# Joining two visits of layer 0's values on TensorE, and moving three steps around them

## The chip, the cores and the metric

The kernel runs on one core of one Trainium2 chip. The metric is the time of one execution on the device in microseconds; lower is better. Times are given as the median of a few runs. A profile is one further execution, recorded by the hardware.

A core has several engines that run side by side and wait for each other through semaphores: TensorE (PE, matrix products, with weight loads counted apart as PEld), VectorE (DVE), ScalarE (ACT), GpSimd (POOL), and SyncE (SP), which here issues the DMA transfers. Each engine takes its instructions in the order of the program.

## The reference, cut to what matters

64 graphs of 256 nodes with 512 features each, an adjacency matrix for each graph, 8 heads of 64. Two layers follow each other; each ends in a residual sum and a layer norm.

```python
# layer 0: graph attention with additive logits
feats  = einsum('bnf,hfu->bhnu', X, W)
e_self, e_neigh = feats . a_self, feats . a_neigh
dense  = leaky_relu(e_self[:, None] + e_neigh[None, :], 0.2) - 1e10 * (1 - A)
out    = relu(softmax(dense) @ feats + b)
x      = layernorm(x + out)
# layer 1: dot-product attention plus adjacency and distance terms
q, k, v = split(x @ W_qkv)
attn   = 0.33 * softmax(q k^T / 8) + 0.33 * adj + 0.33 * exp(-adj)
x      = layernorm(x + (attn @ v) @ W_out + b_out)
```

## The kernel before, in words

All arithmetic is in float32, and everything of one graph stays in SBUF. The 64 graphs pass through a software pipeline written out by hand: in stage b, layer 0's attention of graph b stands beside layer 1's projections of graph b-1 (`attention0_beside_projections1`, L1141), and then layer 1's attention of graph b-1 and b-2 stands beside layer 0's projection of graph b+1 (`attention1_beside_projections0`, L1220). `start()` (L1047) does graph 0 in another way, since the weights of layer 1 are still on their way and layer 0's attention vectors have still to be folded into its weights. `end()` empties the pipeline. The function `do` (L1039) emits one step and then calls `in_order` (L86), which chains every new instruction to the one before it on its engine: the order in the source is the order on each engine.

**Seven products for eight.** The projections of both layers use a Strassen-like scheme of seven block products p1 to p7 (`seven`, L289). Three PSUM banks hold them (L284): p1, p6, p7 and p4 accumulate one on the other in the bank "chain", and after each one ScalarE copies the bank out (L309); p2 has the bank "alone"; p5 and then p3 accumulate in the bank "pair". VectorE adds "alone" or "pair" to what was copied (L312): add 11 uses p2, add 22 uses p5, add 12 uses p5 and p3. So p4 may begin only when p7's copy is out, and p3 only when add 22 has read the bank. For q and k (`pq_p`) a product is 16 records of 128 columns; for v (`pv_p`) and for layer 0 (`pf_p`) it is 4 records of 256 and 264 columns.

**Layer 0's attention.** The exponential of a sum of two logits is split in a row factor and a column factor. `rows` (L482) transposes the row logits with TensorE (four records, `pr`), takes their maximum, exponentiates them (ScalarE, L491), clips them (VectorE, L494) and sends the row to DRAM and back as a broadcast to all partitions (tiles `gs` and `gb`, SP, L498 and L499). `columns` (L541) starts with the subtraction `nd` (VectorE, L543), which waits for that broadcast, and ends in two exponentials on ScalarE. For each of 8 heads, `scaled` multiplies the features by the column factor (ScalarE, two instructions, L610) and `weights` builds the masked weights `pT` (VectorE, two instructions, L646). `product(g, t)` (L657) multiplies weights and features on TensorE for four heads and one tile of 128 nodes: 32 records that use the array as two halves of 64 columns each. `norm0` (L677) divides by the sums, `end` adds the residual.

**Layer 1's attention.** `scores` (TensorE L813, ScalarE L822), `both` (VectorE L834), `sums` (TensorE L842, `pd`), `invert` (VectorE, L863 to L875, then `rs` and `rb`, a second broadcast through DRAM); two graphs later `weights` (VectorE, L901 and L908), `values` (TensorE L918), `residual` (VectorE L996) and `project` (TensorE L1003, with its sum on VectorE, L931).

The order of one stage today, where the change touches it: q/k p1, p2, `columns`, p6, scaling and weights of heads 0 to 3, the store of graph b-3 (two normalisations on ScalarE, L367), add 11, p5, p7, add 22, `product(0, .)`, scaling of heads 4 to 7, p4, weights of heads 4 to 7, `norm0(0, .)`, `attend1` weights 0, p3, add 12, load of a later graph, `product(1, .)`, v's p1, p2, `norm0(1, .)`. The tiles `pT` of all heads rotate through four buffers of one tag.

Of the kernel before, what the change touches and what calls it, by code (L numbers as in the profile page):

```python
# [8 lines left out]
FT = mybir.dt.float32  # L9
BF = mybir.dt.bfloat16  # L10
U8 = mybir.dt.uint8
AF = mybir.ActivationFunctionType
# [5 lines left out]
def kernel(  # L18
# [410 lines left out]
    def proj0(b):  # L429
# [52 lines left out]
        def rows():  # L482
            pr = ps_tile([H, 2, N], f"pr_{b}")
            for s in range(2):
                for t in range(T):
                    transpose(pr[:, s, t * P : (t + 1) * P], V0[b][:, t, :, U + s])
            grow = small.tile([H, N + 1], FT, tag="grow", name=f"grow_{b}", bufs=1)
            nb = small.tile([H, 1], FT, tag="nb", name=f"nb_{b}", bufs=2)
            nc.vector.tensor_reduce(grow[:, N : N + 1], pr[:, 1, :], AX.X, ALU.max)
            nc.vector.tensor_scalar_mul(nb, grow[:, N : N + 1], -0.8)  # L490
            nc.scalar.activation(  # L491
                grow[:, :N], pr[:, 0, :], AF.Exp, bias=nb, scale=-0.8
            )
            nc.vector.tensor_scalar(  # L494
                grow[:, :N], grow[:, :N], 1.0, TINY, op0=ALU.min, op1=ALU.max
            )
            gs = dram.tile([H, N + 1], FT, tag="gs", name=f"gs_{b}")
            nc.sync.dma_start(gs, grow)  # L498
            nc.sync.dma_start(  # L499
                gb.rearrange("p h n -> p (h n)"),  # L500
                gs.rearrange("h n -> (h n)").partition_broadcast(P),
            )
# [105 lines left out]
        def scaled(h):  # L608
# [16 lines left out]
            xT_rows=from_rows,  # L625
            aT=lambda: transpose_blocks(pa, ADJB[b]),
            rows=rows,
            columns=columns,
            far=far,
            shared=shared,  # L630
# [7 lines left out]
    def attend0(b):  # L638
        pT = {}

        def weights(h):

            tag = "pT" if b > 1 or h < HG else "p" if h < HG + 2 else "both"
            pT[h] = work.tile([P, T, N], FT, tag=tag, name=f"pT_{b}_{h}", bufs=4)
            for j in range(T):
                nc.vector.scalar_tensor_tensor(  # L646
                    pT[h][:, j, :],
                    GB[b][h],
                    CCOL[b][:, j, h : h + 1],
                    AT[b][:, j, :],  # L650
                    op0=ALU.max,
                    op1=ALU.mult,
                )

        AV = {}

        def product(g, t):  # L657


            if t == 0:  # L660
                AV[g] = psum.tile([P, T, F], FT, tag="sc", name=f"av0_{b}_{g}", bufs=2)
            av = AV[g][:, t, : HG * UA].rearrange("p (h u) -> p h u", u=UA)
            half = P // 2
            for k in range(HG):
                h = g * HG + k
                for j in range(T):
                    for r in range(2):
                        i = t * P + r * half
                        matmul(  # L669
                            av[r * half : (r + 1) * half, k, :],  # L670
                            pT[h][:, j, i : i + half],
                            V0[b][:, j, h, :UA],
                            start=(j == 0),
                            stop=(j == T - 1),
                        )

        def norm0(g, t):  # L677
            if b not in X1:
                X1[b] = io.tile([P, T, F], FT, tag="x1", name=f"x1_{b}", bufs=3)
            av = AV[g][:, t, : HG * UA].rearrange("p (h u) -> p h u", u=UA)  # L680
            rec = small.tile([P, HG], FT, tag="rec", name=f"rec0_{b}_{g}_{t}")
            nc.vector.reciprocal(rec, av[:, :, U])
            s = slice(g * HG * U, (g + 1) * HG * U)
            nc.vector.tensor_mul(
                X1[b][:, t, s].rearrange("p (h u) -> p h u", u=U),
                av[:, :, :U],
                rec.unsqueeze(2).to_broadcast([P, HG, U]),
            )

        def end(ts=slice(0, T)):  # L690
            if ts.start == 0:
                NORM["l0", b] = LayerNorm(X1[b], b, "l0")
            ln = NORM["l0", b]
            for t in range(ts.start, ts.stop):
                nc.vector.scalar_tensor_tensor(
                    X1[b][:, t, :],
                    X1[b][:, t, :],
                    0.0,
                    X[b][:, t, :],
                    op0=ALU.max,  # L700
                    op1=ALU.add,
                    accum_out=ln.sums[:, t : t + 1],
                )
            ln.mean(ts)
            if ts.stop == T:
                X.pop(b)

        return dict(
            weights=weights,
            product=product,  # L710
            norm0=norm0,
            end=end,
            squares=lambda *ts: NORM["l0", b].squares(*ts),
            norm=lambda *ts: NORM["l0", b].apply(*ts),
        )
# [323 lines left out]
    def do(stage, b, step, *args):  # L1039

        if 0 <= b < NB:
            if (stage, b) not in S:
                S[stage, b] = stages[stage](b)
            S[stage, b][step](*args)
            in_order()

    def start():  # L1047
# [12 lines left out]
        attention_vectors(0, 0)  # L1060
        attention_vectors(1, 0)
        do("proj0", 0, "maxima")
        attention_vectors(0, 1)
        do("turned", 1, "xT")
        do("proj0", 0, "columns")
        do("proj0", 0, "factors")
        attention_vectors(1, 1)
        attention_vectors(0, 2)
        attention_vectors(1, 2)
        attention_vectors(2, 0)  # L1070
        attention_vectors(3, 0)
        for h in range(2):
            do("proj0", 0, "scaled", h)
            do("attend0", 0, "weights", h)
        attention_vectors(2, 1)
        attention_vectors(3, 1)
        attention_vectors(2, 2)
        attention_vectors(3, 2)
        for h in range(2, HG):
            do("proj0", 0, "scaled", h)  # L1080
            do("attend0", 0, "weights", h)
        do("proj0", 1, "features", 0, 0)
        do("proj0", 1, "features", 0, 1)
        do("attend0", 0, "product", 0, 0)
        do("attend0", 0, "product", 0, 1)
        for h in range(HG, H):
            do("proj0", 0, "scaled", h)
            do("attend0", 0, "weights", h)
        do("proj0", 1, "features", 1, 0)
        do("attend0", 0, "product", 1, 0)  # L1090
        do("attend0", 0, "product", 1, 1)
        do("proj0", 1, "features", 1, 1)
        do("attend0", 0, "norm0", 0, 0)
        do("attend0", 0, "norm0", 0, 1)
        combine_weights1(0)
        do("attend0", 0, "norm0", 1, 0)
        do("attend0", 0, "end", tiles[0])
        do("attend0", 0, "squares", tiles[0])
        do("attend0", 0, "norm0", 1, 1)
        do("attend0", 0, "end", tiles[1])  # L1100
        do("attend0", 0, "squares", tiles[1])
        do("attend0", 0, "norm", tiles[0])
        for t in range(T):
            for g in range(2):
# [36 lines left out]
    def attention0_beside_projections1(b):  # L1141


        if b > 1:
# [9 lines left out]
            do("proj1", b - 1, "qk_add", 11)  # L1154
            do("proj1", b - 1, "qk", "p5")
            do("proj1", b - 1, "qk", "p7")
            do("proj1", b - 1, "qk_add", 22)
        do("attend0", b, "product", 0, 0)
        do("attend0", b, "product", 0, 1)
        if b > 1:  # L1160
            for h in range(HG, H):
                do("proj0", b, "scaled", h)
            do("proj1", b - 1, "qk", "p4")
            for h in range(HG, H):
                do("attend0", b, "weights", h)
        do("attend0", b, "norm0", 0, 0)
        do("attend0", b, "norm0", 0, 1)
        do("attend1", b - 2, "weights", 0)
        if b > 1:
            do("proj1", b - 1, "qk", "p3")  # L1170
            do("proj1", b - 1, "qk_add", 12)
        else:
            do("turned", b + 1, "xT")
            do("turned", b + 1, "xC")
            do("proj0", b, "shared")
# [3 lines left out]
            in_order()  # L1179
        if b + 2 < NB:  # L1180
            load(b + 2)
        do("attend0", b, "product", 1, 0)
        do("attend0", b, "product", 1, 1)
        do("proj1", b - 1, "values", "p1")
        do("proj1", b - 1, "values", "p2")
        do("attend0", b, "norm0", 1, 0)
        do("attend0", b, "norm0", 1, 1)
# [1 line left out]
        do("proj1", b - 1, "v_add", 11)  # L1189
        do("proj1", b - 1, "values", "p6")  # L1190
        do("proj1", b - 1, "values", "p5")
        do("attend1", b - 2, "weights", 1)
        do("proj1", b - 1, "values", "p7")
        do("proj1", b - 1, "v_add", 22)
        do("proj0", b + 1, "product", "p1")
# [24 lines left out]
    def attention1_beside_projections0(b):  # L1220
# [10 lines left out]
        for g in range(HG):  # L1231
            do("attend1", b - 2, "values", g)
        do("softmax1", b - 1, "scores", 2)
        do("softmax1", b - 1, "both", 2)
        do("softmax1", b - 1, "scores", 3)
        do("softmax1", b - 1, "both", 3)
        do("attend1", b - 2, "residual")
        do("attend1", b - 2, "project", 0)
        do("proj0", b + 1, "rows")
        do("proj1", b, "hT")  # L1240
        do("attend1", b - 2, "project", 1)
        do("softmax1", b - 1, "sums")
# [119 lines left out]
```

## Time and profile before

| | us |
|---|---|
| median of 3 runs | 2990.16 (2987.5 to 2992.53) |
| profiled execution, its own time | 2991.16 |
| its span in the profile | 2989.4 |
| TensorE busy | 2957.4 |
| VectorE busy | 2610.0 |
| ScalarE busy | 1478.2 |

In the lines of the profile a time in us from the span's start comes first, then the time that the group of instructions took, the engine, the line of the kernel, the operation, output and inputs, shapes and the count; in square brackets stands how long the engine sat idle before it and what released it. In the list of waits the three numbers are the total in us, the number of times and the longest. The busy share of TensorE counts overlapping matmuls once and says little on how well it is used; the distance from one instruction's start to the next says more.

### The profile page before, as it was taken

The page shows a single profiled execution, that of the slowest core. Times are in us where ns is not written, and L with a number is a line of the kernel's source. Part 1 is how long each engine was busy: PE and PEld are TensorE (multiplying, and loading weights), DVE is VectorE, ACT ScalarE, POOL GpSimd, SP SyncE. Part 2 cuts the span into 40 slices and gives each one's busy share as a digit, 9 for nine tenths or more (in the row PEclk, how much of TensorE's full clock was granted, in tenths as well). Part 3 has the DMA queues.
Part 4 walks back from the last instruction along what each step waited for, and adds up shares of the span by engine and source line. Part 5 has one row for each costly group of instructions (what it writes and reads, how often), then busy time and mean ns, then how long its engine had stood idle before and what let it go on. Part 6 is the DMA issues. An engine that isn't in the chain of part 4 may idle for free.

```text
span 2989.4 us, 64730 instructions
## 1 busy us (share of the span) xinstructions
PE 2957.4 (99%) x25526; PEld 2332.6 (78%) x25526; DVE 2610.0 (87%) x5151; ACT 1478.2 (49%) x3585; POOL 183.5 (6%) x526
## 2 busy tenths in 40 slices
PE   8899999999999999999999999999999999999998
PEld 7777877877878778778778778788787787787775
DVE  5889888889888888888888888888988988888885
ACT  2454554455455455455545544554554555455443
POOL 0000000000000000000000000000000000000000
PEclk7999999999999999999999999999999999999999
DMA  6353454444444444444534544444444435445431
GB/s 120 86 128 99 109 130 98 111 126 104 111 122 103 116 109 107 125 102 110 129 96 109 133 97 111 122 104 115 110 108 123 108 105 129 97 108 133 96 93 50
DMA packets 760613, 328.22 MB, mean 110 GB/s; under 512 B 693516, under 2 KB 694268, under 8 KB 744312
## 3 DMA queue, kind: packets, MB, share of 16 engines
q1 hardware_dynamic: 758200, 323.55, 43.5%
q8 instruction: 204, 3.34, 0.5%
q14 instruction: 97, 0.79, 0.1%
q10 hardware_dynamic: 2112, 0.52, 0.1%
HBM read 256.13 MB, written 67.61 MB: 108 GB/s over the span
## 4 chain that ended last, share of the span: by engine, by line
PE 92%; DVE 3%; DMA 3%; ACT 1%; issue 1%; SPq 0%; POOL 0%; DVEq 0%; POOLq 0%
PE pq_p L300 25%; PE po L1003 14%; PE pf_p L300 13%; PE pv_p L300 12%; PE pz L813 8%; PE av L669 8%; PE av L918 7%; PE pd L842 2%; DMA gb<-gs 1%; PE pr L82 1%; DMA out_dram<-x 1%; DVE p L908 0%; DVE p L901 0%; PE pg L532 0%; DMA gs<-grow 0%
## 5 line engine op out<-in xcount | busy, mean ns | idle before, releaser
L300 PE MATMUL pq_p<-hC,wqk_sb 128*128 128x128 f32 x4096 | 487.1, 277 | 2.0 <-ACT qk L309 1.9
L300 PEld LDWEIGHTS pq_p<-hC,wqk_sb 128*128 128x128 f32 x4096 | 468.9, 192 | 7.7 <-ACT qk L309 2.9
L1003 PE MATMUL po<-wo_sb,oT 128*128 128x512 f32 x1024 | 466.3, 599 | 0.0
L646 DVE SCALAR_TENSOR_TENSOR pT<-gb,ccol,at 128x256 f32<-128x256 f32 x992 | 403.2, 480 | 17.6 <-ACT ccol L550 17.6
L300 PEld LDWEIGHTS pq_p<-hT,wqk_sb 128*128 128x128 f32 x3072 | 355.9, 193 | 29.6 <-DVE hC L278 23.9
L300 PE MATMUL pq_p<-hT,wqk_sb 128*128 128x128 f32 x3072 | 373.6, 278 | 3.2 <-DVE hT L121 1.9
L822 ACT ACTIVATE p<-pz,hide 128x512 f32<-128x512 f32 x512 | 310.8, 691 | 123.9 <-PE av L918 106.7
L1003 PEld LDWEIGHTS po<-wo_sb,oT 128*128 128x128 f32 x1024 | 184.7, 190 | 207.5 <-issue 205.8
L309 ACT COPY v<-pv_p 128x256 f32<-128x256 f32 x256 | 95.5, 373 | 472.6 <-PE pv_p L300 472.5
L351 ACT ACTIVATE junk<-x,nmean_l 128x512 bf16<-128x512 f32 x256 | 185.6, 725 | 279.9 <-POOL nmean_l L346 275.8
L908 DVE TENSOR_TENSOR p<-p,ct 128x1024 f32<-128x1024 f32 x252 | 308.7, 1225 | 8.6
L901 DVE TENSOR_TENSOR p<-p,rb 128x1024 f32<-128x1024 f32 x252 | 304.5, 1208 | 5.2 <-DMA rb<-rs 5.2
L669 PE MATMUL av<-v,pT 128*64 128x65 f32 x8192 | 267.1, 223 | 0.6 <-DVE pT L646 0.6
L669 PEld LDWEIGHTS av<-v,pT 128*64 128x64 f32 x8192 | 249.3, 138 | 16.5 <-issue 1.4
L610 ACT ACTIVATE v<-v 128x64 f32<-128x64 f32 x1024 | 260.3, 342 | 0.0
L813 PE MATMUL pz<-qk 64*128 64x256 f32 x2048 | 256.2, 389 | 0.6 <-ACT p L822 0.5
L300 PE MATMUL pf_p<-wf_sb,xC 128*128 128x264 f32 x992 | 252.3, 387 | 0.0
L300 PE MATMUL pv_p<-wv_sb,hC 128*128 128x256 f32 x1024 | 244.4, 381 | 5.5 <-DVE v L312 5.3
L813 PEld LDWEIGHTS pz<-qk 64*128 64x128 f32 x2048 | 187.1, 186 | 65.1 <-ACT p L822 25.6
L918 PE MATMUL av<-p,v 128*64 128x256 f32 x2016 | 231.7, 382 | 0.0
L300 PEld LDWEIGHTS pv_p<-wv_sb,hC 128*128 128x128 f32 x1024 | 193.4, 190 | 37.8 <-DVE v L312 10.7
L309 ACT COPY qk<-pq_p 128x512 f32<-128x512 f32 x256 | 147.7, 577 | 141.5 <-PE pq_p L300 141.4
(137 smaller groups left out, 3806.2 us busy)
## 6 DMA issues: line engine op xcount, KB each, us to landing
rb<-rs SPq DMA_DIRECT2D x63, 1024.0 KB, 4.6
gb<-gs SPq DMA_DIRECT2D x62, 1028.0 KB
xb<-in_x_dram SPq DMA_DIRECT2D x252, 128.0 KB, 4.1
x<-in_x_dram SPq DMA_DIRECT2D x63, 512.0 KB
hs<-x SPq DMA_DIRECT2D x63, 512.0 KB
hb<-hs SPq DMA_DIRECT2D x252, 128.0 KB, 3.4
out_dram<-x SPq DMA_DIRECT2D x63, 512.0 KB, 4.4
adj<-in_adj_dram SPq DMA_DIRECT2D x256, 64.0 KB, 4.5
```

Source lines behind the costliest of these rows:

```text
L300: matmul(d, lhsT, rhs, start=(p in FIRST and i == 0), stop=(i == len(todo) - 1), skip_group_check=True,)
L309: nc.scalar.copy(out[COPIES[p]], dst)
L351: nc.scalar.activation(junk, self.src[:, t, :], AF.Square, bias=self.nmean[:, t : t + 1], accum_out=self.rstd[:, t : t + 1],)
L610: nc.scalar.activation(V0[b][:, t, h, :U], V0[b][:, t, h, :U], AF.Copy, scale=V0[b][:, t, h, U : U + 1],)
L646: nc.vector.scalar_tensor_tensor(pT[h][:, j, :], GB[b][h], CCOL[b][:, j, h : h + 1], AT[b][:, j, :], op0=ALU.max, op1=ALU.mult,)
L669: matmul(av[r * half : (r + 1) * half, k, :], pT[h][:, j, i : i + half], V0[b][:, j, h, :UA], start=(j == 0), stop=(j == T - 1),)
L813: matmul(pz[:, r, j, :], QK[b][rows, g, 1, j * P : (j + 1) * P], QK[b][rows, g, 0, :], start=True, stop=True,)
L822: nc.scalar.activation(p[:, :, j, :], pz[:, :, j, :], AF.Exp, bias=hide[:, j, b : b + 1], scale=U**-0.5,)
L901: nc.vector.tensor_mul(p, p, REC[b][:, k : k + 2, g // 2, :] .unsqueeze(2) .to_broadcast([P, 2, T, N]),)
L908: nc.vector.tensor_add(p, p, CT[b].unsqueeze(1).to_broadcast([P, 2, T, N]))
L918: matmul(av[0][r * U : (r + 1) * U, g % 2, :], V1[b][:, j, 2 * g + r, :], PROBS[b][g][:, r, j, :], start=(j == 0), stop=(j == T - 1),)
L1003: matmul(po, oT[:, c, t * P : (t + 1) * P], wo_sb[:, c, :], start=(c == 0), stop=(c == C - 1),)
```

## The change

Three edits, in the author's words: layer 0's values in one visit with v's first product between q and k's last; row logits ahead of output; the first graph's values ahead of columns.

1. In the stage of graph b (b > 1), the weights of heads 4 to 7 now follow p7 directly, ahead of add 22. After add 22 come `attend1` weights 0, v's p1, then q/k p4 and p3 and add 12, and only then all four `product` steps, one after the other. `attend1` weights 1 move from between v's p5 and p7 to behind the products, ahead of `norm0`. So that eight weight tiles can live at once, heads 4 to 7 use the buffers of the tag "both".
2. `rows` is cut in two. The transposes and the maximum now come right behind the last scores, ahead of `both` 2 and 3; the new step `broadcast` (exponential, clip, the two DMAs) comes behind `both` 3 and ahead of `residual` and `project(0)`. Before, all of it stood behind `project(0)`.
3. In `start()`, graph 0's scaling, weights, values, norms and sums come right behind `factors`, ahead of most of the steps of the attention vectors and of the features of graph 1. Its last weight tile uses the buffer of `rec1`.

The core of the diff:

```diff
             nc.vector.tensor_scalar_mul(nb, grow[:, N : N + 1], -0.8)
+            ROW.update(logits=pr, rows=grow, shift=nb)
+
+        def broadcast():
+            grow = ROW["rows"]
             nc.scalar.activation(
-                grow[:, :N], pr[:, 0, :], AF.Exp, bias=nb, scale=-0.8
+                grow[:, :N], ROW["logits"][:, 0, :], AF.Exp, bias=ROW["shift"], scale=-0.8
             )
...
-            tag = "pT" if b > 1 or h < HG else "p" if h < HG + 2 else "both"
-            pT[h] = work.tile([P, T, N], FT, tag=tag, name=f"pT_{b}_{h}", bufs=4)
+            tag = "pT" if h < HG else "both" if b > 1 or h > HG + 1 else "p"
+            if (b, h) == (0, H - 1):
+                pT[h] = work.tile([P, T, N], FT, tag="rec1", name=f"pT_{b}_{h}", bufs=1)
+            else:
+                pT[h] = work.tile([P, T, N], FT, tag=tag, name=f"pT_{b}_{h}", bufs=4)
...
         do("proj0", 0, "maxima")
-        attention_vectors(0, 1)
         do("turned", 1, "xT")
         do("proj0", 0, "columns")
         do("proj0", 0, "factors")
+        for h in range(H):
+            do("proj0", 0, "scaled", h)
+            do("attend0", 0, "weights", h)
+        for g in range(2):
+            for t in range(T):
+                do("attend0", 0, "product", g, t)
+        for t in range(T):
+            for g in range(2):
+                do("attend0", 0, "norm0", g, t)
+            do("attend0", 0, "end", tiles[t])
+            do("attend0", 0, "squares", tiles[t])
+        attention_vectors(0, 1)
         attention_vectors(1, 1)
+        attention_vectors(2, 0)
+        attention_vectors(3, 0)
         attention_vectors(0, 2)
         attention_vectors(1, 2)
...
+        combine_weights1(0)
         attention_vectors(2, 1)
         attention_vectors(3, 1)
         attention_vectors(2, 2)
         attention_vectors(3, 2)
...
+        for t in range(T):
+            for g in range(2):
+                do("proj0", 1, "features", t, g)
         do("attend0", 0, "norm", tiles[0])
...
             do("proj1", b - 1, "qk", "p5")
             do("proj1", b - 1, "qk", "p7")
-            do("proj1", b - 1, "qk_add", 22)
-        do("attend0", b, "product", 0, 0)
-        do("attend0", b, "product", 0, 1)
-        if b > 1:
             for h in range(HG, H):
                 do("proj0", b, "scaled", h)
+                do("attend0", b, "weights", h)
+            do("proj1", b - 1, "qk_add", 22)
+            do("attend1", b - 2, "weights", 0)
+            do("proj1", b - 1, "values", "p1")
             do("proj1", b - 1, "qk", "p4")
-            for h in range(HG, H):
-                do("attend0", b, "weights", h)
+            do("proj1", b - 1, "qk", "p3")
+            do("proj1", b - 1, "qk_add", 12)
+        for g in range(2):
+            for t in range(T):
+                do("attend0", b, "product", g, t)
+        do("attend1", b - 2, "weights", 1)
         do("attend0", b, "norm0", 0, 0)
         do("attend0", b, "norm0", 0, 1)
...
         do("softmax1", b - 1, "scores", 2)
+        do("softmax1", b - 1, "scores", 3)
+        do("proj0", b + 1, "rows")
         do("softmax1", b - 1, "both", 2)
-        do("softmax1", b - 1, "scores", 3)
         do("softmax1", b - 1, "both", 3)
+        do("proj0", b + 1, "broadcast")
         do("attend1", b - 2, "residual")
         do("attend1", b - 2, "project", 0)
-        do("proj0", b + 1, "rows")
         do("proj1", b, "hT")
```

More of the change, by code (lines that the diff above doesn't have):

```diff
@@ L627, in proj0 @@
             rows=rows,
+            broadcast=broadcast,
             columns=columns,
@@ L1066, in start @@
         do("proj0", 0, "factors")
+        for h in range(H):
[10 more added lines that the diff above has]
+        attention_vectors(0, 1)
         attention_vectors(1, 1)
+        attention_vectors(2, 0)
+        attention_vectors(3, 0)
         attention_vectors(0, 2)
         attention_vectors(1, 2)
[L1070 to L1074, printed above, removed]
+        combine_weights1(0)
         attention_vectors(2, 1)
@@ L1078, in start @@
         attention_vectors(3, 2)
[L1079 to L1085, printed above, removed]
-        for h in range(HG, H):
[L1087 to L1101, printed above, removed]
+        for t in range(T):
+            for g in range(2):
+                do("proj0", 1, "features", t, g)
         do("attend0", 0, "norm", tiles[0])
@@ L1156, in attention0_beside_projections1 @@
             do("proj1", b - 1, "qk", "p7")
-            do("proj1", b - 1, "qk_add", 22)
-        do("attend0", b, "product", 0, 0)
-        do("attend0", b, "product", 0, 1)
-        if b > 1:
             for h in range(HG, H):
                 do("proj0", b, "scaled", h)
+                do("attend0", b, "weights", h)
+            do("proj1", b - 1, "qk_add", 22)
+            do("attend1", b - 2, "weights", 0)
+            do("proj1", b - 1, "values", "p1")
             do("proj1", b - 1, "qk", "p4")
-            for h in range(HG, H):
-                do("attend0", b, "weights", h)
+            do("proj1", b - 1, "qk", "p3")
[4 more added lines that the diff above has]
+        do("attend1", b - 2, "weights", 1)
         do("attend0", b, "norm0", 0, 0)
         do("attend0", b, "norm0", 0, 1)
[L1168 to L1172, printed above, removed]
+        if b == 1:
             do("turned", b + 1, "xT")
@@ L1181, in attention0_beside_projections1 @@
             load(b + 2)
-        do("attend0", b, "product", 1, 0)
-        do("attend0", b, "product", 1, 1)
-        do("proj1", b - 1, "values", "p1")
+        if b == 1:
+            do("proj1", b - 1, "values", "p1")
         do("proj1", b - 1, "values", "p2")
@@ L1191, in attention0_beside_projections1 @@
         do("proj1", b - 1, "values", "p5")
-        do("attend1", b - 2, "weights", 1)
         do("proj1", b - 1, "values", "p7")
```

## The prediction, made before the result was known

> **What bounds the kernel now.** I read the page first, then the repeat of a graph in the stream of TensorE, then the streams of the other engines around the edited steps.
>
> The page:
>
> ```profile
> span 2989.4 us, 64730 instructions
> PE 2957.4 (99%) x25526; PEld 2332.6 (78%) x25526; DVE 2610.0 (87%) x5151; ACT 1478.2 (49%) x3585; POOL 183.5 (6%) x526
> PE 92%; DVE 3%; DMA 3%; ACT 1%; issue 1%; SPq 0%; POOL 0%; DVEq 0%; POOLq 0%
> ```
>
> TensorE sets the time, in work and in the chain that ended last. From the start of one q/k block to the next it repeats in 45.36 us (47 of the 62 distances; the others but the first and last are longer by 0.1 to 1.6). An edit counts, then, by what it does to TensorE's gaps, times about 61 graphs. Below is one ordinary graph, whose q/k block starts at 2388.28; I call that moment 0. Timeline of TensorE:
>
> ```profile
> 2388.28 3.84 PE L300 MATMUL pq_p<-hT,wqk_sb 128*128 128x128 f32 x32
> 2391.96 5.52 PE L300 MATMUL pq_p<-hC,wqk_sb 128*128 128x128 f32 x48
> 2397.41 2.09 PE L669 MATMUL av<-v,pT 128*64 128x65 f32 x64
> 2399.43 2.05 PE L300 MATMUL pq_p<-hC,wqk_sb 128*128 128x128 f32 x16
> 2401.32 1.95 PE L300 MATMUL pq_p<-hT,wqk_sb 128*128 128x128 f32 x16
> 2403.20 2.09 PE L669 MATMUL av<-v,pT 128*64 128x65 f32 x64
> ```
>
> Layer 0's values (L669) come in two visits, with q/k's p4 and p3 between. The visits are what the change joins. Next VectorE (DVE) and then ScalarE (ACT) in the same stretch:
>
> ```profile
> 2388.30 0.69 DVE L931 SCALAR_TENSOR_TENSOR x<-po,x 128x512 f32<-128x512 f32 x1
> ...
> 2388.90 0.71 DVE L863 STREAM_TRANSPOSE zd<-pd 128x512 f32<-128x512 f32 x1
> ...
> 2392.68 0.18 DVE L543 TENSOR_TENSOR nd<-v,gb 128x16 f32<-128x16 f32 x1
> 2393.15 3.26 DVE L646 SCALAR_TENSOR_TENSOR pT<-gb,ccol,at 128x256 f32<-128x256 f32 x8 [0.28 <-ACT ccol L550]
> 2396.32 0.69 DVE L312 TENSOR_TENSOR qk<-pq_p,qk 128x512 f32<-128x512 f32 x1
> 2398.38 0.69 DVE L312 TENSOR_TENSOR qk<-pq_p,qk 128x512 f32<-128x512 f32 x1 [1.37 <-ACT qk L309]
> 2398.98 3.25 DVE L646 SCALAR_TENSOR_TENSOR pT<-gb,ccol,at 128x256 f32<-128x256 f32 x8
> ```
>
> ```profile
> 2393.94 0.59 ACT L309 COPY qk<-pq_p 128x512 f32<-128x512 f32 x1 [0.71 <-PE pq_p L300]
> 2394.43 2.03 ACT L610 ACTIVATE v<-v 128x64 f32<-128x64 f32 x8
> 2396.36 1.51 ACT L367 ACTIVATE x<-x,shift_l,rstd_l 128x512 f32<-128x512 f32 x2
> 2397.78 0.56 ACT L309 COPY qk<-pq_p 128x512 f32<-128x512 f32 x1
> ```
>
> Two things to see. The copy of q/k's p7 ends only at 10.06, since eight scalings and two normalisations stand ahead of it on ScalarE. And the add after it (the second L312) reads the bank "pair", on which p3 accumulates next. So p4 waits for the copy (same bank, "chain") and p3 for that add; today the first visit (9.13 to 11.15) hides both.
>
> **What the Trainium skill says.** "TensorEngine Tiling (Array Packing)", Key Properties: "Changing tiling mode (not just tile) drains the TensorE". The trace agrees. Starts of q/k records are 112 ns apart, of value pairs (two 64-column halves) 58.5; the step from q/k into a visit is 205 and the first step inside it 107; the step out is 152 and the next q/k step 213. Over the usual steps that is 93 + 49 ns going in and 94 + 101 coming out: 0.34 us for each visit. "TensorE: Matmul & The Clock Gate", Part 1, says the clock follows the activity of windows of about 3.4 us. The granted clock agrees: 0.50 from 21.5 to 45.4 us, 1.00 from 120 to 2980. The joined visit lasts 3.9 us, so it matters that the values count as activity: the stretch 82.9 to 86.4, mostly values, kept 1.00.
>
> **The change, part by part**
>
> *One visit in place of two.* Removed: one switch in and out, -0.34 us a graph. V's p1 between q/k products keeps the 128x128 mode; v and layer 0's projections alternate today at their plain 216 and 222 ns steps, so I cost that at nothing.
>
> *p4's wait.* Between p7 and p4 only v's p1 is left: four records of 216 ns, 0.86. p7's last record starts at 8.92, the next slot is 9.03, so p4 could start at 9.90. ScalarE's order up to the p7 copy is unchanged and starts from p6's end on TensorE, so the copy still ends at 10.06. A weight load that waits starts 0.05 after the release (77.37 to 77.42 at another graph's p7), and the load is then exposed for 0.10 (213 in place of 112). So p4 starts at 10.11: +0.32.
>
> *p3's wait.* The second half of the weights (L646, eight instructions) now stands ahead of the add on VectorE. From the row sums' transpose (L863) the order is fixed: 3.79 to nd, 0.46 to the weights, 3.17, the add 0.60, 3.17, the add's 0.69: 11.88 in all. L863 starts at 0.62 today. The moved row logits take it earlier: ahead of hT only residual and project 0's sum remain, and by the same durations hT starts at -3.7 in place of -2.7; the sum of project 1 then waits for its product (about -0.87), and L863 waits for pd, whose last record ends at 0.07: 0.13. The add ends at 12.01 and releases p3's load at 12.06. Behind p4, p3's load would come at 11.90: +0.06, and +0.10 exposed.
>
> Sum for one graph: -0.34 + 0.32 + 0.16 = +0.14; 61 graphs (3 to 63): +8.5. What follows has cover: the joined visit starts at 14.06 with its scalings done by 12.0 (ACT) and its weights by 11.3; both L901/L908 pairs fit on VectorE beside p3 and the visit, and the norms end by 20.9 for v's second half, where today they end at 20.2 and TensorE does not wait. If that cover failed, each us late would be a us a graph.
>
> *Row logits earlier.* The four transposes move, their 0.44 us and the switches next to them stay. Queued behind nothing new: gs and gb go out on SP after the mask's DMA, before rs, as now, but 2.7 us earlier (gb at -4.0 in place of -1.3). This removes a wait:
>
> ```profile
> DVE nd L543 <- DMA gb<-gs: 10.9, 9, 2.8
> ```
>
> The distances over 45.36 from the third graph on add up to 4.3 us, and the largest (1.59) is the graph in which nd waited 2.0. gb lands near 4.1 today, against nd at 4.4; then near 1.1 against 3.9. I take -4.3.
>
> *Tags.* The weights of heads 4 to 7 use the four buffers of "both", which the row sums have read by 0.1; needed at 8.2: nothing.
>
> *Graph 1* saves one switch, -0.3.
>
> *The start.* TensorE is busy from 23.8 to 54.35 almost without a gap, most of it at half clock. The factors start 2.0 earlier (two attention-vector products, 1.8, and a wait of 1.3 go behind). But the values come near 29, where the clock is 0.50: up to 7.6 us in place of 4.0; then TensorE waits about 2.6 for norms, sums and the small copies that now stand behind them on VectorE; the features run later, half of them at the low clock as now; and after the features the column step no longer waits for the sums, about -1.3. Bounds -2 and +5; I take +2, since which windows raise the clock cannot be read off.
>
> Sum against the profiled execution (2991.16, its span 2989.4): 2991.2 + 8.5 - 4.3 - 0.3 + 2 = 2997. The median of the runs lies 1.0 below: **2996**.
>
> **Rivals**
>
> *The new waits are longer.* If L863 doesn't move forward (something in VectorE's tail is later than I count, or gb lands after 3.9), the add ends at 12.5 and each graph costs +0.62: +38 - 4 + 2, near 3025. For it: 11.9 us of VectorE in a row with no gap, then an exact race with p3. Against: L863's forerunners have 0.3 us to spare.
>
> *The switch is gained in full.* If the copy ended by 9.84 and the add by 11.63, the graphs would save 0.34 each: -21 - 4, near 2966, faster. One mechanism, one place: ScalarE's copy of p7. Against: 1.5 us of normalisation stands ahead of it and nothing in the change moves it. A much better start (-5) could also end below 2984.
>
> *Nothing to gain in joining.* If the joined visit paid a switch again where the group of heads changes, each graph would be at +0.48, near 3017. Against: inside a visit today, where the head and the tile change, no step is longer than the others.
>
> **How the numbers follow.** A difference under 0.2% (6 us) is about what can't be told from no change. The forecast has 0.60, with a range of its own from 2985 to 3008: it straddles +0.2%, so 0.03 faster, 0.32 same, 0.25 slower. Longer waits, the third rival included, 0.25, all slower. The full gain 0.15: 0.13 faster, 0.02 same. In all 0.16, 0.34, 0.50. The range leaves out most of the full gain and the tail above the longer waits: 2983 to 3028.
>
> **What would show it.** One visit of 128 value records a graph with steps of 58.5 ns throughout; p4's load released by ScalarE's copy and p3's by VectorE's add, in the list of waits at about 60 each; L863 near 0.13; nd's waits for gb gone; the repeat at 45.5. A repeat of 45.0 would make me wrong towards faster, one above 45.8 towards slower; so would a clock below 1.00 after 120 us, or a first q/k block far from 59.5.

## The result, and the profile after

The changed kernel takes 2992.41 us (median of 12 runs, 2986.8 to 2995.24), the kernel before 2990.19 beside it (12 runs). The ratio is 1.0006, with a 95% interval from 0.9997 to 1.0015: no difference that can be measured. The forecast was 2996. The profiled execution took 2993.09 us, its span is 2991.3. So a large edit left the time where it was, and the question is where the 0.34 us a graph went that the joined visits were to save.

The repeat, from one q/k block to the next, went from 45.363 to 45.400 us (medians of the 62 distances from graph 2's stage on). The spans split as follows.

| part of the span | before | after | difference |
|---|---|---|---|
| to the q/k block of graph 2's stage | 113.90 | 114.81 | +0.9 |
| stage of graph 2 | 47.39 | 49.24 | +1.9 |
| stage of graph 3 | 45.71 | 45.40 | -0.3 |
| stages of graphs 4 to 62 | 2680.69 | 2679.79 | -0.9 |
| stage of graph 63 | 40.82 | 41.33 | +0.5 |
| the rest | 60.85 | 60.75 | -0.1 |

In the fourth row two things stand against each other: 59 repeats that are longer by 0.037 (+2.2), and the distances above the repeat (what single distances exceed it by, summed), which fell from 4.3 to 1.2 us (-3.1).

The timeline of TensorE after the change, for a graph whose q/k block starts at 1935.68 (moment 0 below):

```profile
1935.68 3.84 PE L300 MATMUL pq_p<-hT,wqk_sb 128*128 128x128 f32 x32
1939.36 5.52 PE L300 MATMUL pq_p<-hC,wqk_sb 128*128 128x128 f32 x48
1944.72 1.03 PE L300 MATMUL pv_p<-wv_sb,hT 128*128 128x256 f32 x4
1945.78 2.05 PE L300 MATMUL pq_p<-hC,wqk_sb 128*128 128x128 f32 x16
1947.75 2.05 PE L300 MATMUL pq_p<-hT,wqk_sb 128*128 128x128 f32 x16
1949.73 3.95 PE L678 MATMUL av<-v,pT 128*64 128x65 f32 x128
1953.61 1.13 PE L300 MATMUL pv_p<-wv_sb,hT 128*128 128x256 f32 x4
```

The visit is one, of 128 records. But v's p1 takes four records of 216 ns, 0.86, and the next line begins 1.06 after it: p4 waited. The 16 records of p4 and of p3 take 1.97 and 1.98 where the plain step of 112 ns gives 1.79; of p3's excess, 0.09 is the switch into the visit. The two engines that p4 and p3 wait for, VectorE first, then ScalarE:

```profile
1935.82 0.72 DVE L872 STREAM_TRANSPOSE zd<-pd 128x512 f32<-128x512 f32 x1 [0.27 <-PE pd L851]
...
1939.61 0.18 DVE L547 TENSOR_TENSOR nd<-v,gb 128x16 f32<-128x16 f32 x1
1940.07 3.26 DVE L655 SCALAR_TENSOR_TENSOR pT<-gb,ccol,at 128x256 f32<-128x256 f32 x8 [0.28 <-ACT ccol L554]
1943.24 0.68 DVE L312 TENSOR_TENSOR qk<-pq_p,qk 128x512 f32<-128x512 f32 x1
1943.84 3.25 DVE L655 SCALAR_TENSOR_TENSOR pT<-gb,ccol,at 128x256 f32<-128x256 f32 x8
1947.01 0.68 DVE L312 TENSOR_TENSOR qk<-pq_p,qk 128x512 f32<-128x512 f32 x1
```

```profile
1943.75 1.51 ACT L367 ACTIVATE x<-x,shift_l,rstd_l 128x512 f32<-128x512 f32 x2
1945.16 0.57 ACT L309 COPY qk<-pq_p 128x512 f32<-128x512 f32 x1
```

The copy of p7 ends at 10.05 and p4 starts at 10.10; add 22 ends at 12.01 and p3 starts at 12.065. Each starts 0.05 after its release. In the list of waits (engine, line, releaser; total us, times, longest):

```profile
PEld pq_p L300 <- ACT qk L309: 28.8, 65, 0.9
PEld pq_p L300 <- DVE qk L312: 4.5, 4, 2.5
DVE nd L547 <- DMA gb<-gs: 3.4, 2, 2.4
DVE zd L872 <- PE pd L851: 17.1, 61, 0.6
```

The first line is p4's wait: once a graph, where before it came 5 times. The wait of p3 is too short to be listed for an ordinary graph: p3 starts at 12.065, and at 11.98 in a kernel below in which its add comes early. The third line is the broadcast of the row logits: nd waited for it twice in place of nine times. The fourth says that the row sums' transpose now waits for TensorE, where VectorE was late for it before.

### The profile page after: what moved, and what is told of

The parts are those of the page before. It is cut to its first block, busy times and chain, and to the rows that moved or that the text cites. A ratio compares the mean times of both kernels' runs of the same rounds, so it can differ in the third digit from the quotient of the medians.

```text
span 2991.3 us, 63550 instructions
## 1 busy us (share of the span) xinstructions
PE 2952.2 (99%) x25526; PEld 2322.8 (78%) x25526; DVE 2610.3 (87%) x5151; ACT 1468.4 (49%) x3585; POOL 184.6 (6%) x526
## 4 chain that ended last, share of the span: by engine, by line
PE 95%; DVE 2%; DMA 1%; ACT 0%; issue 0%; SPq 0%; POOL 0%; DVEq 0%; POOLq 0%
PE pq_p L300 27%; PE po L1012 14%; PE pv_p L300 13%; PE pf_p L300 13%; PE av L678 8%; PE pz L822 8%; PE av L927 7%; PE pd L851 2%; PE pr L82 1%; DVE pT L655 1%; DMA gb<-gs 0%; PE pg L536 0%; PE pf L583 0%; PE pwa L404 0%; DMA gs<-grow 0%
## 5 line engine op out<-in xcount | busy, mean ns | idle before, releaser
L300 PEld LDWEIGHTS pq_p<-hC,wqk_sb 128*128 128x128 f32 x4096 | 469.0, 192 | 29.1 <-ACT qk L309 28.8
L1012 PE MATMUL po<-wo_sb,oT 128*128 128x512 f32 x1024 | 450.0, 592 | 0.0
L678 PE MATMUL av<-v,pT 128*64 128x65 f32 x8192 | 254.7, 223 | 0.7 <-DVE pT L655 0.6
L822 PEld LDWEIGHTS pz<-qk 64*128 64x128 f32 x2048 | 187.1, 186 | 66.7 <-ACT p L831 27.3
L300 PEld LDWEIGHTS pf_p<-wf_sb,xC 128*128 128x128 f32 x992 | 188.9, 191 | 31.7
```

The lines of the kernel that those rows point to most:

```text
L300: matmul(d, lhsT, rhs, start=(p in FIRST and i == 0), stop=(i == len(todo) - 1), skip_group_check=True,)
L678: matmul(av[r * half : (r + 1) * half, k, :], pT[h][:, j, i : i + half], V0[b][:, j, h, :UA], start=(j == 0), stop=(j == T - 1),)
L822: matmul(pz[:, r, j, :], QK[b][rows, g, 1, j * P : (j + 1) * P], QK[b][rows, g, 0, :], start=True, stop=True,)
L1012: matmul(po, oT[:, c, t * P : (t + 1) * P], wo_sb[:, c, :], start=(c == 0), stop=(c == C - 1),)
```

## The experiments

The theory, from the prediction: the joined visit saves 0.34 us a graph, p4's wait for ScalarE's copy and p3's for VectorE's add take it back, and they stand one behind the other on TensorE, so that of two waits only what the later one leaves is paid. The main rivals: each wait costs its own share; joining saves nothing. Four kernels first, each an edit of the changed one.

**Normalisations later.** ScalarE's copy of p7 comes earlier; no other step is moved in the source.

```diff
-            do("attend1", b - 3, "store")
             do("proj1", b - 1, "qk_add", 11)
             do("proj1", b - 1, "qk", "p5")
             do("proj1", b - 1, "qk", "p7")
+            do("attend1", b - 3, "store")
```

> The changed kernel, with the store of graph b-3 (two normalisations on ScalarE) behind q/k's p7 in place of ahead of it, so that the copy of p7 ends near 9.8 in place of 10.04. Theory: the two waits stand one behind the other on TensorE and the later one, p3's for add 22 (12.06), decides; p4 starts near 9.9 in place of 10.10 and p3 still at 12.06: 2992, within 3 us of the changed kernel. Rival: each wait costs its own share, and the copy is the larger one: 0.3 less a graph, near 2974.

Measured: 2992.27 us, ratio to before 1.0005 (0.9997 to 1.0014); repeat 45.400, the same in all its digits. The copy ends at 9.82 in place of 10.04, p4 starts at 9.90 in place of 10.10, and p3 at 12.065 as before. What p4 waits less, p3 waits more; in the list of waits of this kernel:

```profile
PEld pq_p L300 <- DVE qk L312: 23.1, 62, 2.5
PEld pq_p L300 <- ACT qk L309: 16.8, 66, 1.5
```

62 waits for the add, where the changed kernel lists 4; the waits for the copy fell from 28.8 to 16.8 us. The rival (2974) falls: the larger wait, taken alone, is worth nothing.

**Add 22 first.** VectorE does the add ahead of the weights of heads 4 to 7.

```diff
+            do("proj1", b - 1, "qk_add", 22)
             for h in range(HG, H):
                 do("proj0", b, "scaled", h)
                 do("attend0", b, "weights", h)
-            do("proj1", b - 1, "qk_add", 22)
```

> The changed kernel, with add 22 ahead of the weights of heads 4 to 7 on VectorE, so that it ends near 10.8 in place of 12.01. Theory: p4 still waits for the copy (10.10), p3 follows it without a wait: 0.18 less a graph, near 2981. Rival, each wait its own share: 0.16 less, the same here; it parts from the theory in the two kernels beside this one. A third reading, that VectorE alone holds the graph back: 0.4 less or more, under 2970.

Measured: 2976.55 us, 0.9951 (0.9935 to 0.9968). The repeat is 45.216, 0.184 less, as expected (0.18); p4 still starts at 10.09 and p3 at 11.98. The time fell by 4 us more than expected, because the stage of graph 2 also lost its wait for the add (46.9 in place of 49.2), the stage of graph 63 fell by 1.0, and the distances above the repeat (1.2) went.

**Both.** The two edits at once.

> Both edits together: normalisations behind p7 and add 22 ahead of the weights of heads 4 to 7. Theory: p4 at 9.87, p3 right behind it; 0.41 less a graph than in the changed kernel, near 2967, so more than the two edits alone add up to. Rival: the sum of the two alone.

Measured: 2964.79 us, 0.9905 (0.989 to 0.9921). The repeat is 44.996: 0.404 less than in the changed kernel, where the two edits alone gave 0.000 and 0.184. p4 starts at 9.90 and p3 at 11.76. That the whole is more than twice the sum shows that the waits stand in series.

**Two products of v between.** No order on ScalarE or VectorE changes; TensorE only does more of its own work before it asks.

```diff
             do("proj1", b - 1, "values", "p1")
+            do("proj1", b - 1, "values", "p2")
             do("proj1", b - 1, "qk", "p4")
...
         if b == 1:
             do("proj1", b - 1, "values", "p1")
-        do("proj1", b - 1, "values", "p2")
+            do("proj1", b - 1, "values", "p2")
```

> The changed kernel, with v's p2 as well as p1 between q/k's p7 and p4; ScalarE and VectorE keep their order. Theory: p4 comes at 10.76 and p3 at 12.55, both behind what they wait for, and the joined visit keeps its whole gain: 0.48 less a graph, a repeat near 44.9, near 2963. Rival: joining the visits gains nothing by itself, or the weights and norms on VectorE become the limit: 2985 or more.

Measured: 2962.9 us, 0.9902 (0.9888 to 0.9917); repeat 44.920, 0.48 less, as expected. The timeline of TensorE in this kernel (the q/k block starts at 1915.55):

```profile
1924.58 1.89 PE L300 MATMUL pv_p<-wv_sb,hT 128*128 128x256 f32 x8
1926.31 1.95 PE L300 MATMUL pq_p<-hC,wqk_sb 128*128 128x128 f32 x16
1928.10 1.95 PE L300 MATMUL pq_p<-hT,wqk_sb 128*128 128x128 f32 x16
1929.98 3.95 PE L678 MATMUL av<-v,pT 128*64 128x65 f32 x128
```

v's products take 1.73, p4 and p3 1.79 and 1.88: the plain steps, the last with the switch into the visit. The copy still ends at 10.04 and the add at 12.01, and p4 (10.76) and p3 (12.55) come behind both. Here the change's own gain is seen whole: the repeat is 0.44 under that of the kernel before, 0.34 for the visit and 0.10 for the row logits (below). It also shows what was left in the kernel with both edits, 0.076 more: there p4's load still waits for the copy, and p4's first step takes 186 ns, here 109.

The next four take the change apart.

**Row logits put back** (edit 2 undone in the changed kernel).

> The changed kernel with the row logits put back behind project 0, in one step as before. Theory: the row sums' transpose on VectorE comes at 0.62 again in place of 0.13, the whole run up to add 22 with it, so p3 starts near 12.55 in place of 12.06 (+0.49), and project 0 again takes an exposed load of 128 columns behind the scores (+0.10); the broadcast lands later and each lateness now reaches p3: 0.6 less gained a graph, 3030 to 3038. Rival: the moved logits only helped the broadcast, and the repeat stays near 45.4: 2993 to 2997.

Measured: 3037.69 us, 1.0165 (1.0151 to 1.0179). The repeat is 45.979 (+0.58), the row sums' transpose (L863 before the change) starts at 0.62, add 22 ends at 12.49, p3 starts at 12.54. Its list of waits:

```profile
PE pq_p L300 <- DVE qk L312: 35.3, 62, 2.2
```

This is the first rival of the prediction, with its mechanism and its price. The distances above the repeat add up to 10.2 us in place of 1.2: in the twelve graphs after graph 3 whose distance is longer, by 0.09 to 1.74, it is longer by what nd was late, within 0.02. Without slack on VectorE a late broadcast reaches TensorE in full.

**Row logits alone** (edit 2 made in the kernel before).

> The kernel before with the moved row logits alone. Theory: the repeat falls by the 0.10 of the exposed load, to 45.26, and the late broadcasts of before (about 4 us in all) go: near 2980. Rival: TensorE's work is the same in another order, only the broadcasts count: near 2986.

Measured: 2983.65 us, 0.9977 (0.9969 to 0.9985), between the two. The repeat, 45.264, decides for the theory: 0.10 less. But the distances above the repeat only fell from 4.3 to 2.8 us, though nd waited for a broadcast once in place of nine times. What is left of them is another wait, on a line that both kernels list; that of this experiment:

```profile
DVE x L689 <- DMA out_dram<-x: 11.2, 21, 1.0
```

The norms of layer 0 (`norm0`) write a buffer whose earlier contents are still on their way to DRAM. In the kernel before, eight of the twelve long distances after graph 3 had nd in time, within 0.1 us, and the norms late; three (1.6, 0.5 and 0.4) had nd late by 1.7 to 2.0; one of 0.2 had neither. In the eight, and in the three too, the distance is longer by the lateness of the norms less 0.4 us, which is what they have to spare. The changed kernel starts the norms 2.3 us later in the graph (16.2 in place of 13.9), and its list of waits doesn't have this wait.

**The visit split again.** v's p2 goes between the two halves.

```diff
-        for g in range(2):
-            for t in range(T):
-                do("attend0", b, "product", g, t)
+        for t in range(T):
+            do("attend0", b, "product", 0, t)
+        if b > 1:
+            do("proj1", b - 1, "values", "p2")
+        for t in range(T):
+            do("attend0", b, "product", 1, t)
...
-        do("proj1", b - 1, "values", "p2")
+            do("proj1", b - 1, "values", "p2")
```

> The changed kernel with v's p2 put between the two halves of the joined visit; nothing else moves. Theory: one more switch in and out, 0.34 a graph, a repeat of 45.74: near 3013. Rival: the visits' number costs nothing by itself: 2992.

Measured: 3011.85 us, 1.0074 (1.0059 to 1.0089); repeat 45.747, +0.347. The price of a visit is what single records of the kernel before gave (0.34).

**The start of before** (edit 3 undone in the changed kernel).

> The changed kernel with the start (graph 0) of the kernel before. Theory: the two starts differ by less than they scatter, because the same start code put the first q/k product between 56.2 and 63.3 us in the profiles so far: 2987 to 2993. Rival: the new start costs the 2 us forecast and the old one takes them back: 2990 or a little under with an interval clear of the changed kernel.

Measured: 2992.57 us, 1.0005 (0.9998 to 1.0011), no different from the changed kernel. One profile says little on the start: the new one put the first q/k product at 56.2, 57.1, 60.7, 61.6, 62.1, 62.3, 63.3 and 63.3 us in the profiles with it, the old one at 56.1, 59.1 and 59.5.

**The version that beats both.** V's p2 ahead of p4 and add 22 ahead of the weights.

> The changed kernel with v's p2 ahead of p4 and add 22 ahead of the weights of heads 4 to 7, both. Theory: no wait was left in the repeat of the kernel with v's p2 alone, so the repeat stays at 44.92; only graph 2, in which the late broadcast holds add 22 back, can gain, up to 3 us: 2959 to 2963. Rival: with the waits gone something else gives way too, and the repeat falls under 44.9.

Measured: 2960.62 us, 0.9901 (0.9883 to 0.992), 1% under the kernel before. The repeat is 44.920 again. The stage of graph 2 takes 47.0 in place of 50.2, and that of graph 63 40.4 in place of 41.0. The 2.3 us between the two medians, of four runs each, are not clear of the scatter (2959.8 to 2962.1 against 2961.7 to 2963.7); the two stages are read from one profile each.

## Why the prediction was right, and where it was off

- *What bounds the kernel* and *one visit in place of two*: right. Split and join each moved the repeat by what single records gave.
- *V's p1 keeps the mode*: right. The step into it was 112 ns, its own steps 216, and with v's p2 behind it the step to p4 was plain.
- *p4's wait*: forecast at 10.11, measured 10.10. *p3's wait*: L863 forecast at 0.13, measured 0.14; the add's end 12.01, measured 12.01; p3 12.06, measured 12.065. Together the two waits were forecast at 0.48 a graph, and putting v's p2 ahead of p4 gave back 0.48. The sign that p3's wait would be listed about 60 times did not come: it was listed 4 times. The start of v's second half came out 0.137 later than before, against 0.14.
- *The rival "longer waits"* was the right reading of what holds L863; putting the row logits back made it come true, with a repeat 0.62 above that of the kernel before, as forecast. The time was 3038 against 3025, since the rival let the late broadcasts go (-4), while they grew: 10.2 us above the repeat in place of 4.3, with more on top in the stages of graphs 2 and 3.
- *Row logits earlier*, "their 0.44 us and the switches next to them stay": this step failed. TensorE gained 0.10 a graph here, which is why the repeat is 45.40 and not 45.50: -0.34 for the visit, +0.48 for the two waits and -0.10 here make +0.04, and 0.037 was measured. The timeline of TensorE before, and below it after, from the last scores on:

```profile
2377.85 2.00 PE L813 MATMUL pz<-qk 64*128 64x256 f32 x16
2379.78 3.70 PE L1003 MATMUL po<-wo_sb,oT 128*128 128x512 f32 x8
2383.32 0.60 PE L82 MATMUL pr<-ident,v 128*8 128x128 f32 x4
2383.75 3.60 PE L1003 MATMUL po<-wo_sb,oT 128*128 128x512 f32 x8
2387.28 1.07 PE L842 MATMUL pd<-both,ones 128*32 128x256 f32 x16
```

```profile
1970.75 2.00 PE L822 MATMUL pz<-qk 64*128 64x256 f32 x16
1972.68 0.60 PE L82 MATMUL pr<-ident,v 128*8 128x128 f32 x4
1973.12 7.03 PE L1012 MATMUL po<-wo_sb,oT 128*128 128x512 f32 x16
1980.08 1.07 PE L851 MATMUL pd<-both,ones 128*32 128x256 f32 x16
```

From the first line's successor to pd it was 7.50 us and is 7.40. The switch out of the scores (306 ns from the last score to the next start) is paid in both. The whole difference lies in the first step behind it. Ahead of an output product the weight load has 128 columns; the first step takes 533 ns in place of 429, and the second load starts 108 ns after the first. Ahead of the transposes the load has 8 columns; the first step takes 113 in place of 109, and the second load starts 5 ns after the first (medians of the graphs). So the first load behind the switch isn't hidden here, and the later ones are. The row logits alone, in the kernel before, moved the repeat by the same 0.10. Times 61 that is 6 us, the better part of what was missing; the output was judged by its plain steps, and its first one was there to be read.

- *Tags*, nothing: right. The weights of heads 4 to 7 start at 8.16 without idle time before them.
- *Removes a wait*, -4.3: the size was about right (-3.1 in this profile; graph 9's broadcast was still late by 1.0), its cause only in part. I put all long distances down to nd. Three of them, 2.5 of 4.3 us, were nd; most of the others were the norms' wait for the store, as the row logits alone showed.
- *The sum for graphs 3 to 63* left graph 2 at nothing. There nd waited for its broadcast, 2.8 before and 2.4 after, and came 3.7 and 3.8 late. Before, 2.0 of that reached TensorE; in the new order p3 waits for add 22, which stands behind nd, and all 3.8 did: +1.9. That follows from the prediction's own chain on VectorE; I had not walked it for this graph.
- *The start*, +2: within the scatter, and not to be told from nothing by the runs. For the same reason a first q/k block far from 59.5, which was to be a sign of being wrong, says nothing: it came at 62.3.

The errors (about -6 and -1, with +1.9 and +1.2) leave the forecast about 4 us high. That it wasn't 7 is luck: errors of both signs met. And the forecast gave a slower kernel 0.50 and no change 0.34, so what came was not what it held likeliest. In the stage of graph 63, longer by half a us, the trace shows scores whose load waits 2.0 us for ScalarE (before, the longest such wait was 0.9), while another gap of TensorE there shrank; why ScalarE is late was not followed up.

## What to carry to other kernels

When work that stood between a producer and its consumer on the bound engine is moved, look up for each consumer behind it what it was hiding, and when that release comes; several releases in series hide each other, so taking away one of them alone can be worth nothing. The cheapest cure here was not to hurry the late engines, but to put more of the bound engine's own independent work ahead of the question: one step moved, for 1%.

Price the order of matmul groups by the first step behind each switch, not by the plain steps: here the group with 8 weight columns was the better first one, by 0.10 us a graph.

## What was not expected of the hardware

The step behind a switch of the array was longer by more, the more columns its weight load had: by 104 ns (533 against 429) and 101 (213 against 112) with 128 columns, by 49 (107 against 58.5) with 64, by 4 (113 against 109) with 8. That the columns set the price is a reading of these four places; the groups differ in their products too, and no run changed the columns alone.

Unchanged start code put the first q/k product anywhere between 56.2 and 63.3 us from one kernel's profile to the next. The granted clock goes with this. In the eight profiles with the new start it stood at 0.50 for 13.7, 17.1, 23.9, 23.9, 27.3, 27.3, 30.7 and 30.7 us ahead of that product, in the order in which the product came later: 56.2, 57.1, 60.7, 61.6, 62.1, 62.3, 63.3 and 63.3. What sets these stretches isn't shown. A busy TensorE alone did not raise the clock: in the kernel before it was 0.50 from 21.5 to 45.4 us, and matmuls fill 23.35 of these 23.90 us in the profile.
